# One batch of key sums per sequence, a fixed order for the first two superblocks, and later loads in a macaron transformer block

## The chip, the core and the metric

The kernel runs on one core of a Trainium2 chip. A core has five engines with instruction queues of their own: TensorE (PE; weight loads are shown as PEld), VectorE (DVE), ScalarE (ACT), GpSimd (POOL) and SyncE (SP), which issues most transfers. Engines wait for each other through semaphores. Products are accumulated in PSUM, eight banks of 128 x 2 KB. The metric is the time of one execution on the device in microseconds, the median of several runs; lower is better.

## What is computed

A macaron block over x of 16 sequences x 256 tokens x 256 features: half a feed-forward step, causal attention with 16 heads of 16 that share 4 key and value groups, and half a feed-forward step again, each on the layer norm of x and added to x. The feed-forward weights are made ternary in the kernel from their own mean absolute value.

```python
def ternary_quant(w):
    scale = jnp.mean(jnp.abs(w)) + 1e-08
    return jnp.clip(jnp.round(w / scale), -1.0, 1.0) * scale

def ffn(x):                      # W_up, W_gate: 1024 x 256, W_down: 256 x 1024
    up, gate = x @ wu.T, x @ wg.T
    return (silu(up) * gate) @ wd.T

def attn(x):
    q, k, v = x @ Wq + bq, x @ Wk + bk, x @ Wv + bv      # k, v repeated for 4 heads each
    scores = where(causal, -inf, q @ k.T / sqrt(16))
    return softmax(scores) @ v

x = x + 0.5 * ffn(layernorm(x))
x = x + attn(layernorm(x))
x = x + 0.5 * ffn(layernorm(x))
```

## The kernel before

Two sequences (512 tokens) make a superblock n = 0 to 7. All of x stays on the chip (`xs`). A pass (n, p) of the feed-forward part is eight units f of 128 hidden features, then four down products of 128 tokens each. `order` lists the sixteen passes: the first six superblocks' first pass, then second passes with the two left first passes between.

Inputs of products are split in a high and a low half-precision part, so a product u or g of a unit is four matmuls of 512 columns (`products`, L467): two halves of the features times high and low. A unit is u, g, a curve th on ScalarE (Silu for the first four passes, Tanh after), a join h on VectorE, and the split of h into hT on ScalarE (high) and GpSimd (low). `ffn_down` (L518) has sixteen matmuls of 256 columns for each 128 tokens.

The attention of a superblock: norm, transposing transfer xT_a, three products `project` (L545), the results sent to DRAM (qd, kd) and loaded again in another layout (`load(q)` for sequence q = 2n + s, four loads of queries and five of keys). `peak` scores a row's maxima, `peak_parts` and `peak_rows` turn them into three extra rows of the queries. `exponents(q, g)` (L696, L697, L705) makes for one group g of four heads three score tiles, their exponentials in a tile pT (128 x 3 x 512, three buffers) and the causal mask. `weighted(q, gp)` (L727) sums values over the keys for two groups: sixteen f32 matmuls on strips of 32 columns of the array; the profile counts 32, as f32 is done in two. `attended` (L743) turns the sums, divides by the sum of the exponentials, and GpSimd adds the result to x.

What sets the order. The program issues steps from several chains (`ffn_chain`, `prepares`, `qkv_chain`, `load_chain`, `peak_chain`, `sequence_chain`). A step has a cost, names of steps that must come before it and a lag in accumulated cost; `run` takes from the attention chains when their share of cost falls behind. The framework then orders each engine's queue by a timeline of its own, save instructions that are pinned with `keep_in_program_order` or have high priority.

At the start the weights come in and are made ternary: `ternary_sums` (absolute sums on ScalarE and VectorE), `ternary_scale` (one matmul with ones adds over the partitions, then scale, upper and lower bound), `ternary_piece` (L336 or L332 and L333: a mask below the lower bound; L337: the compare with the upper bound minus the mask). These steps are entered in `ffn_chain` at fixed places (the list at the end of the function). Filler matmuls (`warm`) come ahead of the first work (12) and of the first and third gate products (NWF, four each). The raw weights lie in the buffers that later hold the queries.

The two lines that say how the sums over the keys are laid out and issued:

```python
groups = (2 * gp, 2 * gp + 1)                 # two of the four groups of heads
steps.append([e[0], e[1], e[2], w[0], e[3], a[0], w[1], a[1]])
```

Of the kernel before, what the change touches and what calls it, by code (L numbers as in the profile page):

```python
# [25 lines left out]
ENG_U = "vvvv"  # L26
ENG_G = "vapa"
ENG_D = "aaaa"
NUF = "000000"
NWF = "404000"  # L30
# [7 lines left out]
NCUT = 4  # L38
PINF = 0
NW4 = 0  # L40
PRE = 0
USUM = 1
GSUM = 0
PING = 0
HPU = 0
GFIRST = 0
PINF1 = 0
TDA = 1
PINK = 1
KM = 2  # L50
KV = 12
PINA = 0
PINM = 1
PINT = 0
NWARM = 12
NWARM2 = 0
NWARM3 = 0
GCUT = 0
# [9 lines left out]
C1 = 1  # L68
C2 = 4
C3 = 5  # L70
TD = 6
DR = 6
DS = 2
PM = 9
LAG_NORM0 = 10.0
DOWN_AT0 = 5
DOWN_GAP0 = 1
GU = 1
QKV_LEAD = 11
LAG_ANORM = 6.0  # L80
LAG_LOAD = 12.0
GAP_PEAK = 1.0
# [11 lines left out]
NORM = 1024.0  # L94


@with_exitstack
def macaron_kernel(
# [56 lines left out]

    x_t = x.rearrange("(n s) (t p) e -> n p (s t) e", s=2, t=2)
# [39 lines left out]
    wqkv = ap_.tile([P, 3, 512], F32, tag="pT", name="wqkv", bufs=3)[:, :EC, : 3 * P]  # L196
# [4 lines left out]
    load_x(0)  # L201
    for w, w_t in ((wu, w_upT), (wg, w_gateT)):
        for i in range(NCUT if w is wu or GCUT else 1):
            nn = NCUT if w is wu or GCUT else 1
            cut = slice(i * F // nn, (i + 1) * F // nn)
            nc.sync.dma_start(w[:, :, cut], w_t.rearrange("(c p) f -> p c f", p=P)[:, :, cut])
    load_x(1)
    nc.sync.dma_start(wd, w_downT.rearrange("(c p) e -> p c e", p=P))

    def load_rest():  # L210
        nc.sync.dma_start(wqkv, w_qkv.rearrange("(c p) f -> p c f", p=P))
        nc.sync.dma_start(bqkv, b_qkv)
        for n in range(2, NSB):
            load_x(n)
# [5 lines left out]
    nc.vector.tensor_copy(identh, ident)  # L220
    ones = const.tile([P, P], F32, tag="ones", name="ones")
    nc.vector.memset(ones, 1.0)
    neg_half = const.tile([P, TT], F32, tag="neg_half", name="neg_half")
    nc.vector.memset(neg_half, -0.5)

    def warm(n, name):
        if n:
            pw = bank([P, P], f"warm_{name}")
            for _ in range(n):
                nc.tensor.matmul(pw, ones, ones, start=True, stop=True)  # L230

    warm(NWARM, "start")

# [3 lines left out]

    box = {}
# [13 lines left out]
    def constant_rows():  # L252


        c = ap_.tile([P, 2, 1536], F16, tag="pT", name="constant_rows", bufs=3)
        k, v = c[:, 0, : NU * U], c[:, 1, :P]
        nc.gpsimd.memset(k[KP:KR], 0.0)
        ku = k[KP:KR].rearrange("p (u k) -> p u k", k=U)
        for at, base in UNDER:
            nc.gpsimd.affine_select(  # L260
                out=ku[:, at : at + 2], in_=ku[:, at : at + 2], pattern=[[0, 2], [-1, U]],
                compare_op=ALU.is_ge, fill=-MASK, base=base, channel_multiplier=1,
            )
        nc.gpsimd.memset(k[KR : KR + 3], -MROW)
        nc.gpsimd.memset(v[KP:KR], 0.0)
        vj = v[KP:KR].rearrange("p (j b) -> p j b", b=4)
        nc.gpsimd.affine_select(
            out=vj, in_=vj, pattern=[[1, 32], [0, 4]], compare_op=ALU.not_equal,
            fill=MASK, base=0, channel_multiplier=-1,
        )  # L270
        for to in Ks:
            nc.sync.dma_start(
                to[KP : KR + 3].rearrange("p g u k -> p g (u k)"),
                k[KP : KR + 3].unsqueeze(1).to_broadcast([KR + 3 - KP, G, NU * U]),
            )
        box["queries"] = v

    def constant_values():
        for v in PARTS:
            nc.gpsimd.memset(v[:, 4 * 6 * G :], 0.0)  # L280
        for v in VT:
            nc.gpsimd.memset(v, 0.0)
            nc.gpsimd.memset(v[:, :, :, D : D + 1], 1.0)
# [9 lines left out]
    def ternary_sums(w, name):  # L293
        if name == "d":
            cuts = [(w[:, : FC // 2], 1), (w[:, FC // 2 :], 1)]
        elif name == "u" or GCUT:
            fq = F // NCUT
            cuts = [(w[:, :, i * fq : (i + 1) * fq], 0 if i % 2 == 0 and not USUM else 1) for i in range(NCUT - 1)]
            h = fq // 2
            cuts += [(w[:, :, (NCUT - 1) * fq : (NCUT - 1) * fq + h], 0), (w[:, :, (NCUT - 1) * fq + h :], 1)]  # L300
        else:
            cuts = [(w[:, : EC // 2], GSUM), (w[:, EC // 2 :], 1)]
        part = small.tile([P, len(cuts)], F32, tag="part", name=f"part_{name}")
        for i, (piece, on_scalar) in enumerate(cuts):
            if on_scalar:
                junk = fp.tile([P] + list(piece.shape[1:]), F16, tag="th", name=f"junk_{name}_{i}")
                nc.scalar.activation(junk, piece, AF.Abs, accum_out=part[:, i : i + 1])
            else:
                pin(PING and name == "g", nc.vector.tensor_reduce(
                    part[:, i : i + 1], piece, AX.XY, ALU.add, apply_absolute_value=True  # L310
                ))
        return part

    def ternary_scale(w, name, part):
        n = w.shape[1] * w.shape[2]
        allsum = bank([P, part.shape[1]], f"allsum_{name}")
        nc.tensor.matmul(allsum, ones, part, start=True, stop=True)
        tot = small.tile([P, 1], F32, tag="tot", name=f"tot_{name}")
        nc.vector.tensor_reduce(tot, allsum, AX.X, ALU.add)
        s = const.tile([P, 1], F32, tag=f"s_{name}", name=f"s_{name}")  # L320
        nc.vector.tensor_scalar(s, tot, 1.0 / (P * n), TERNARY_EPS, ALU.mult, ALU.add)
        hi = small.tile([P, 1], F32, tag="hi", name=f"hi_{name}")
        nc.vector.tensor_scalar(hi, s, 0.5, None, ALU.mult)
# [799 lines left out]
```

## Time and profile before

| | |
|---|---|
| median of 3 runs | 550.11 us (549.1 to 550.27) |
| the profiled execution | 550.52 us |
| its span, first to last instruction | 548.7 us |
| mean granted clock of TensorE | 0.991 |
| L518, down products | 1024 matmuls, 121.9 us busy |
| L467, u and g of most passes | 448 matmuls each, 115.3 and 115.0 us |
| L696, scores for the exponentials | 192, 54.0 us |
| L727, sums over the keys | 1024, 49.1 us (329 ns mean) |
| L697, exponentials on ScalarE | 192, 120.1 us (696 ns mean) |
| L734, copies of the sums on ScalarE | 64 of 256 elements, 22.1 us |

A row of the timeline gives the start, the duration, the engine, the line of the kernel, the operation, the output and its inputs, the shape, and how many instructions were merged; in brackets stands idle time of the engine just before, and what ended it. Durations of merged matmuls overlap those of the next row, since matmuls are pipelined: what a group costs is read from its start to the next start. In the groups, a line has the count, the busy time and the mean of one. The slices on the page are of 13.7 us each, in tenths.

### The profile page before, as it was taken

The page shows a single profiled execution, that of the slowest core. Times are in us where ns is not written, and L with a number is a line of the kernel's source. Part 1 is how long each engine was busy: PE and PEld are TensorE (multiplying, and loading weights), DVE is VectorE, ACT ScalarE, POOL GpSimd, SP SyncE. Part 2 cuts the span into 40 slices and gives each one's busy share as a digit, 9 for nine tenths or more (in the row PEclk, how much of TensorE's full clock was granted, in tenths as well). Part 3 has the DMA queues.
Part 4 walks back from the last instruction along what each step waited for, and adds up shares of the span by engine and source line. Part 5 has one row for each costly group of instructions (what it writes and reads, how often), then busy time and mean ns, then how long its engine had stood idle before and what let it go on. Part 6 is the DMA issues. An engine that isn't in the chain of part 4 may idle for free.

```text
span 548.7 us, 11537 instructions
## 1 busy us (share of the span) xinstructions
PE 530.2 (97%) x4273; PEld 328.7 (60%) x4273; DVE 434.8 (79%) x1027; ACT 375.3 (68%) x658; POOL 355.1 (65%) x384
## 2 busy tenths in 40 slices
PE   5899998989999999999999999999999999999997
PEld 4446555646655656755656656666645666566565
DVE  5988988978898899887578898678966799647753
ACT  5785847576767957797675678856698445875642
POOL 4357789656569777688555579746589443866542
PEclk7899999999999999999999999999999999999999
DMA  8923258463017527325625404660026720020201
GB/s 283 308 62 59 39 130 179 118 159 75 1 28 193 93 78 170 66 42 153 148 50 140 95 8 82 173 129 5 1 40 135 174 62 19 23 59 11 67 30 48
DMA packets 128017, 51.20 MB, mean 93 GB/s; under 512 B 102069, under 2 KB 127705, under 8 KB 127961
## 3 DMA queue, kind: packets, MB, share of 16 engines
q1 hardware_dynamic: 127529, 50.08, 38.1%
q8 instruction: 33, 0.54, 0.4%
q10 hardware_dynamic: 432, 0.39, 0.3%
q14 instruction: 23, 0.19, 0.1%
HBM read 22.41 MB, written 14.68 MB: 68 GB/s over the span
## 4 chain that ended last, share of the span: by engine, by line
PE 68%; DVE 12%; ACT 5%; DMA 5%; POOL 4%; issue 3%; SPq 2%; DVEq 0%; POOLq 0%; ACTq 0%
PE d L518 15%; PE u L467 13%; PE g L467 13%; PE o L727 8%; PE st L696 6%; PE s L630 5%; PE qkv L545 4%; DVE tops L645 2%; PE ot L743 2%; DMA qd<-sp 1%; DVE h L497 1%; DMA kd<-sp 1%; POOL hT L508 1%; ACT pT L697 1%; POOL xparts_f L383 1%
## 5 line engine op out<-in xcount | busy, mean ns | idle before, releaser
L508 POOL TENSOR_TENSOR hT<-h,hT 128x512 f16<-128x512 f32 x128 | 148.7, 1167 | 77.2 <-ACT hT L507 77.0
L697 ACT ACTIVATE pT<-st,exp_scale 128x512 f32<-128x512 f32 x192 | 120.1, 696 | 21.0 <-PE st L696 20.8
L507 ACT CAST hT<-h 128x512 f16<-128x512 f32 x128 | 79.7, 623 | 67.2 <-DVE h L502 49.1
L518 PE MATMUL d<-td,hT 128*128 128x256 f16 x1024 | 121.9, 273 | 0.5 <-DVE sp L570 0.4
L705 POOL TENSOR_SCALAR_AFFINE_SELECT pT<-pT 128x512 f32<-128x512 f32 x128 | 80.7, 636 | 58.5 <-ACT pT L697 57.8
L467 PE MATMUL u<-xT_f,tu 128*128 128x512 f16 x448 | 115.3, 379 | 0.4 <-DVE h L502 0.3
L467 PE MATMUL g<-xT_f,tg 128*128 128x512 f16 x448 | 115.0, 379 | 0.0
L645 DVE TENSOR_REDUCE tops<-s 128x8 f32<-128x512 f32 x160 | 103.4, 680 | 11.1 <-PE s L630 10.9
L518 PEld LDWEIGHTS <-hT 128*128 128x128 f16 x1024 | 98.9, 98 | 19.2 <-issue 0.9
L501 DVE SCALAR_TENSOR_TENSOR tmp<-th,u 128x512 f32<-128x512 f32 x96 | 65.7, 684 | 40.2 <-ACT th L499 39.7
L499 ACT ACTIVATE th<-u,half_u 128x512 f32<-128x512 f32 x96 | 66.6, 694 | 38.1 <-PE u L467 36.3
L467 PEld LDWEIGHTS <-tg 128*128 128x128 f16 x512 | 49.9, 98 | 63.1 <-DVE tg L337 2.9
L467 PEld LDWEIGHTS <-tu 128*128 128x128 f16 x512 | 47.1, 98 | 44.1 <-issue 2.0
L502 DVE SCALAR_TENSOR_TENSOR h<-g,tmp 128x512 f32<-128x512 f32 x96 | 65.6, 684 | 5.4 <-PE u L467 0.3
L696 PE MATMUL st<-Qs,ks 99*128 99x512 f16 x192 | 54.0, 380 | 3.4 <-ACT pT L697 2.0
L630 PEld LDWEIGHTS <-Qs 96*128 96x128 f16 x576 | 47.2, 114 | 11.6 <-issue 3.0
L630 PE MATMUL s<-ks,Qs 96*128 96x64 f16 (+3 forms) x576 | 50.2, 227 | 0.1
L727 PE MATMUL o<-pT,vt 128*32 128x128 f32 (+1 forms) x1024 | 49.1, 329 | 0.1
L523 DVE SCALAR_TENSOR_TENSOR x<-d,so,x 128x256 f32<-128x256 f32 x64 | 30.4, 477 | 20.2 <-PE d L518 19.7
L727 PEld LDWEIGHTS o<-pT,vt 128*32 128x32 f32 x1024 | 28.8, 109 | 23.9 <-issue 8.1
L383 POOL TENSOR_TENSOR xparts_f<-xn_f,xparts_f 128x1024 f16<-128x1024 f32 x14 | 29.8, 2130 | 9.6 <-ACT xparts_f L380 7.7
L545 PE MATMUL qkv<-xT_a,wparts 128*128 128x512 f16 x144 | 34.0, 379 | 1.8 <-DMA xT_a<-xparts_a 1.6
(164 smaller groups left out, 603.6 us busy)
## 6 DMA issues: line engine op xcount, KB each, us to landing
qd<-sp SPq DMA_DIRECT2D x32, 256.0 KB, 2.8
Qs<-qd SPq DMA_DIRECT2D x64, 128.0 KB, 3.6
x<-in_x SPq DMA_DIRECT2D x8, 512.0 KB, 8.8
ks<-kd SPq DMA_DIRECT2D x64, 64.0 KB, 2.7
out<-x SPq DMA_DIRECT2D x32, 128.0 KB, 2.2
kd<-sp SPq DMA_DIRECT2D x16, 128.0 KB, 2.8
ks<-kd SPq DMA_DIRECT2D x16, 128.0 KB, 2.9
Qs<-in_w_upT SPq DMA_DIRECT2D x4, 256.0 KB
```

The lines of the kernel that those rows point to most:

```text
L467: nc.tensor.matmul(acc, w[:, c, f * P : (f + 1) * P], ffn_ready[key][:, a, c, :], start=(c == 0 and a == 0), stop=(c == EC - 1 and a == 1),)
L499: nc.scalar.activation(th, up, AF.Tanh, scale=scales["half_u"])
L501: nc.vector.scalar_tensor_tensor(tmp, th, 1.0, up, ALU.add, ALU.mult)
L507: nc.scalar.copy(hT[:, f, 0, :], h)
L508: nc.gpsimd.tensor_tensor(hT[:, f, 1, :], h, hT[:, f, 0, :], ALU.subtract)
L518: nc.tensor.matmul(acc, hT[:, f, a, t * P : (t + 1) * P], td[:, f, :], start=(f == 0 and a == 0), stop=(f == FC - 1 and a == 1),)
L630: nc.tensor.matmul(sc[:, at : at + n, :], Qs[0:KR, b // 4, g * P : (g + 1) * P, b % 4], strided(k[:, g, place], [(step * U, m) for step, m ...
L645: nc.vector.tensor_reduce(peaks[q][:, u, :], sc, AX.X, ALU.max)
L696: nc.tensor.matmul(sc, keys.rearrange("p u k -> p (u k)"), mov, start=True, stop=True)
L697: nc.scalar.activation(pT[:, u, :].rearrange("p (h b j) -> p h b j", h=4, b=4), sc.rearrange("p (h j b) -> p h b j", h=4, b=4), AF.Exp, sc ...
L705: nc.gpsimd.affine_select(out=v, in_=v, pattern=[[0, 4], [1, P]], compare_op=ALU.is_ge, fill=0.0, base=0, channel_multiplier=-1,)
L727: pin(not first, nc.tensor.matmul(at[:, half * P :], v[:, 2 * s + half, g, :], moving, start=half == 0, stop=half == 1, tile_position=(0, ...
```

## The change

Three parts, each with its edits.

**Sums over the keys.** One batch `weighted(q)` takes all four groups of a sequence; two banks hold two groups each, the order inside the batch is groups 0 and 2, then 1 and 3; pT has four buffers; the copies oT take two groups at once. `sequence_chain` issues four exponent steps, the batch, and the two ends.

```diff
-        pT = ap_.tile([P, 3, 512], F32, tag="pT", name=f"pT_{q}_{g}", bufs=3)
+        pT = ap_.tile([P, 3, 512], F32, tag="pT", name=f"pT_{q}_{g}", bufs=4)
...
-    def weighted(q, gp):
+    def weighted(q):
...
-        groups = (2 * gp, 2 * gp + 1)
-        pT = [probs.pop((q, g)) for g in groups]
-        o = [bank([P, S], f"o_{q}_{g}") for g in groups]
+        pT = [probs.pop((q, g)) for g in range(G)]
+        o = [bank([P, 2, S], f"o_{q}_{gp}") for gp in range(2)]
...
+        for i2 in range(2):
+            for half in range(2):
+                for gp in range(2):
+                    g = 2 * gp + i2
+                    for i in range(4):
+                        cut = slice(i * P, (i + 1) * P)
+                        moving = pT[g][:, 0:2, cut] if half == 0 else pT[g][:, 2, cut]
+                        pin(not first, tensor.matmul(
+                            o[gp][32 * i : 32 * i + 32, i2, half * P :], v[:, 2 * s + half, g, :], moving,
+                            start=half == 0, stop=half == 1, tile_position=(0, 32 * i),
+                        ))
+                        first = False
+        for gp in range(2):
+            oT = ap_.tile([P, 2, S], F32, tag="oT", name=f"oT_{q}_{gp}", bufs=2)
+            scalar.copy(oT, o[gp])
+            sums[q, gp] = oT
...
-            steps.append([e[0], e[1], e[2], w[0], e[3], a[0], w[1], a[1]])
+            steps.append(e + [w] + a)
```

**The first two superblocks.** Everything on VectorE, ScalarE, GpSimd and TensorE up to the end of the second superblock's units, the first superblock's down products, the third superblock's norm, the split of the projection weights and the first attention norm is issued from a table of names, and each engine keeps that order (a wrapper `Engine` pins every instruction). The norm and the unit are cut into their single operations (`EarlyNorm`, `Unit`), and the making of ternary weights is changed: ScalarE writes the absolute values while it sums them (up and gate), the signs (plus or minus a half) are made before the scale is known, and one operation of VectorE compares and multiplies. For the first 256 up and gate columns it comes in two halves. The lower bound, the mask and its subtraction are gone; `HELD` carries the half in the scales. Some sums move to VectorE, all d sums stay on ScalarE. The fillers are 14 ahead of the work, then 2 and 3 inside the table; those before the gate products are gone.

```diff
+ORDER = """
+st0 ag0 st1 rs0 ag1 su0 xn0 rs1 su1 gu0:V tr0 gu1:P xn1 tr1 warm2 gu2:V su2 su3v hi01 gu3:P hi00
+lo01 allu warm3 azu lo00 sg0 oneu cutu peru tu0b tu0a gg2:P U01 sg1 gg0:V tu2 azg U00 th01 tu1
+gg3:P s1b U03 th00 s1a U02 sg1v th03 gg1:P agg1 allg gd3:A tu3 U04 gd2:A cutg misc gd0:A tg3 U07
+rs1x gd1:A tg0b tg0a G01 sd0 tg2 sh1 xV G00 xA1 h01 xA0 G05 tg1 th02 h00 H01 G03 s2a L01 H00 G02
+h03 th04 L00 U05 h02 H03 th07 G04 s2b L03 H02 tr1x th05 h04 L02 G06 h05 hi11 hi10 G07 lo11 H05
+lo10 U06 H04 L05 h07 sd1 U10 most L04 U11 th06 H07 h06 U13 th11 L07 ag2 mt th10 alld G11 ve2 top
+H06 miscd rs2 cutd td1 th13 ev U16 L06 xV2 G17 sh2 h11 xA2 td3 G10 H11 td2 G13 ph2 L11 td0 U17 h10
+th16 pl2 D1 h13 H10 pw H13 th17 D2 L10 END2 h17 ws us L13 D0 H17 r2 wc L17 sa2 D3 r1 wl r0 sa1 sa0
+U14 r3 sa3 G16 th14 aga G12 rsa h16 U15 H16 sha xVa xAa L16 G15 G14 pha U12 h14 th15 pla h15 H14
+th12 H15 h12 ENDa L15 H12 L14 L12
+"""
...
+            def issue(*args, **kwargs):
+                ins = fn(*args, **kwargs)
+                if box["in_order"]:
+                    tc.keep_in_program_order(ins)
+                return ins
...
+    def size_pass(n, c, lo, hi, i=None):
+        scalar.activation(
+            size[n][:, c, lo:hi], raws[n][:, c, lo:hi], AF.Abs,
+            **({} if i is None else {"accum_out": part[n][:, i : i + 1]}),
+        )
...
+    def sums_by_vector(n, c, lo, hi, i):
+        vector.tensor_reduce(
+            part[n][:, i : i + 1], raws[n][:, c, lo:hi], AX.X if isinstance(c, int) else AX.XY, ALU.add, apply_absolute_value=True
+        )
...
+    def half_sign(engine, n, cut):
+        if engine is scalar:
+            scalar.activation(sign[n][cut], raws[n][cut], AF.Sign)
+        else:
+            engine.tensor_scalar(sign[n][cut], raws[n][cut], 0.0, 0.5, ALU.is_ge, ALU.subtract)
...
+    def ternary(n, cut):
+        src = size[n] if n in size else raws[n]
+        vector.scalar_tensor_tensor(tern[n][cut], src[cut], cuts[n], sign[n][cut], ALU.is_gt, ALU.mult)
...
+    by = {"V": vector, "P": gpsimd, "A": scalar}
+    for name in ORDER.split():
+        if name[:4] == "warm":
+            warm(int(name[4:]))
+            continue
+        name, _, engine = name.partition(":")
+        ops[name](*([by[engine]] if engine else []))
+    box["in_order"] = False
+    constant_keys()
```

How to read the table. `Ukf`, `Gkf`: up and gate product of unit f of superblock k; `th`, `h`, `H`, `L`: its curve (ACT), join (DVE), high (ACT) and low (POOL) part. `st`, `ag`, `rs`, `xn`, `tr`, `hi`, `lo`: the first superblock's norm by halves; `s1..`, `xA`, `xV`, `tr1x`: the second's; `s2..` to `END2`: the third's; `sa` to `ENDa`: the first attention norm. `su`, `sg`, `sd`: sums of sizes; `allu`, `allg`, `alld`: the sum over the partitions; `gu0:V`: signs of a quarter of the up weights on VectorE (P: GpSimd, A: ScalarE); `tu`, `tg`, `td`: the ternary weights; `D`, `r`: down product and residual; `most` to `us`: the projection weights.

The loads at the start: x of the first superblock in two halves, the gate weights in two halves instead of one transfer, the rest in the same succession. The vt memsets go from GpSimd to VectorE; the constant rows of the keys are sent after the table (`constant_keys`), those of the queries at place 12 of the chain. In the tanh path the product (th + 1) u is written over th, where it went to a tile of its own.

**Loads of the second sequence.** An odd sequence's loads come a lag after the even one's, for sequence 1 also after the norm of the second superblock's attention; its transposing transfer and those loads are pinned.

```diff
-            need = [(("project", q // 2, 1), 3.0)]
+            need = [(("load", q - 1), LAG_ODD)] if q % 2 else [(("project", q // 2, 1), 3.0)]
+            if q == 1:
+                need.append((("anorm", 1), 1.0))
...
+            pin(name == "a_1", nc.sync.dma_start(xT, parts.rearrange("p a c t e -> p (a c t e)"), transpose=True))
```

`LAG_ODD` is 5. `run` counts the table's feed-forward cost as done when it starts.

## The prediction

> **What bounds the kernel now.** I read the page's busy shares and slices first, to see which engine sets the end and where it is not full.
>
> ```profile
> span 548.7 us, 11537 instructions
> PE 530.2 (97%) x4273; PEld 328.7 (60%) x4273; DVE 434.8 (79%) x1027; ACT 375.3 (68%) x658; POOL 355.1 (65%) x384
> PE   5899998989999999999999999999999999999997
> DVE  5988988978898899887578898678966799647753
> PEclk7899999999999999999999999999999999999999
> ```
>
> TensorE is the bound. From the fourth slice on it is full, so there a change pays only by making TensorE's own work shorter or by taking out a wait of TensorE. The first two slices (13.7 us each) are the only stretch with much idle time, at a reduced clock. Asked by stage, PE is busy 48.13 of the first 57.00 us, 64.02 of 57 to 125, and 372.75 of the 375 us from 125 to 500.
>
> Next, TensorE's timeline of the start.
>
> ```profile
> 9.64 0.59 PE L317 MATMUL allsum_u<-part_u,ones 128*128 128x5 f32 x2 [4.26 <-ACT junk_u L307]
> 11.19 2.03 PE L402 MATMUL xt_first<-ident,xn_first 128*128 128x128 f32 x8 [0.96 <-ACT xn_first L363]
> 13.94 0.61 PE L467 MATMUL u<-xT_first,tu 128*128 128x512 f16 x1
> 14.34 1.92 PE L230 MATMUL warm_g<-ones 128*128 128x128 f32 x8
> 16.05 1.49 PE L467 MATMUL u<-xT_first,tu 128*128 128x512 f16 x3
> 18.69 1.04 PE L467 MATMUL g<-xT_first,tg 128*128 128x512 f16 x4 [1.15 <-DVE tg L337]
> 24.70 1.03 PE L467 MATMUL u<-xT_first,tu 128*128 128x512 f16 x4
> 55.90 1.03 PE L467 MATMUL g<-xT_second,tg 128*128 128x512 f16 x4
> ```
>
> The first product starts at 13.94 and waits in the middle of its four matmuls until 16.05; at 24.70 only three units (six products of four matmuls, u and g of each) are done; the last product of the second superblock starts at 55.90 and the next group starts at 56.76. A product costs 0.863 us at full clock (24.70 to 25.56), so six are 5.2 us.
>
> VectorE's timeline of the same stretch says why.
>
> ```profile
> 13.14 0.74 DVE L337 SCALAR_TENSOR_TENSOR tu<-Qs,hi_u,dn_u 128x512 f16<-128x512 f32 x1
> 13.80 1.40 DVE L348 BATCH_NORM_STATS2 st_second<-x 128x6 f32<-128x256 f32 x4
> 15.11 0.67 DVE L405 TENSOR_TENSOR xT_first<-xt_first,xT_first 128x512 f16<-128x512 f32 x1
> 17.89 0.74 DVE L337 SCALAR_TENSOR_TENSOR tg<-Qs,hi_g,dn_g 128x512 f16<-128x512 f32 x1
> ```
>
> The low part of the first input (L405) runs after work that nobody needs yet: the statistics of the second superblock, and ahead of them 1.20 us of gate sums at 12.02.
>
> Then the sums over the keys in the timeline of TensorE, whole and split:
>
> ```profile
> 123.40 1.03 PE L467 MATMUL g<-xT_f,tg 128*128 128x512 f16 x4
> 124.36 1.51 PE L727 MATMUL o<-pT,vt 128*32 128x256 f32 x32
> 125.80 0.82 PE L696 MATMUL st<-Qs,ks 99*128 99x512 f16 x3
> ```
> ```profile
> 309.22 1.29 PE L727 MATMUL o<-pT,vt 128*32 128x256 f32 x24
> 310.44 0.39 PE L696 MATMUL st<-Qs,ks 99*128 99x512 f16 x1
> 310.76 0.43 PE L727 MATMUL o<-pT,vt 128*32 128x128 f32 x8
> 311.12 0.60 PE L696 MATMUL st<-Qs,ks 99*128 99x512 f16 x2
> ```
>
> A product ends its share of the array at 123.40 + 0.863 = 124.26; the batch starts 0.10 later and the next group starts 1.44 after it: 1.54 us for a batch. Nearly all 32 batches show these numbers. In the split batch, 8 short matmuls cost 0.10 + 0.36 and the other 24 cost 0.10 + 1.22, so a split costs 1.78 - 1.54 = 0.24 us: an entry and an exit are a fixed price, whatever is in the batch.
>
> Last, the queue of loads and the one wait of TensorE on a transfer:
>
> ```profile
> 87.47 4.24 SPq L613 DMA_DIRECT2D ks<-kd  x5
> 91.82 2.25 SPq L388 DMA_TRANSPOSE xT_a<-xparts_a  x1
> ```
> ```profile
> 96.21 1.47 PE L545 MATMUL qkv<-xT_a,wparts 128*128 128x512 f16 x6 [1.58 <-DMA xT_a<-xparts_a]
> ```
>
> **The change, part by part.** The sum starts from the profiled execution: 550.52 us, of which 548.7 are its span; it is 0.41 above the median of the runs, 550.11.
>
> *One batch per sequence.* 32 batches become 16 of twice the matmuls; the same matmuls run, so 16 entries and exits go. By the split batch one is 0.24; a second reckoning: if 32 matmuls alone took the time of their columns at the pace of L467 (512 columns in 0.216 us, four passes for f32, four column strips at once) they took 2 x 0.43 + 2 x 0.215 = 1.29, and 1.54 - 1.29 = 0.25. I take 0.25: **-4.0 us**. Bounds: the visible entry alone, 16 x 0.10 = -1.6; and -4.8, if the three split batches (0.24 each) come whole too. The 64 copies oT (390 ns for 256 elements) become 32 of 512, near the 623 to 696 ns of other ACT passes of 512: 22.1 us become some 21, on an engine at 68%. Nothing there.
>
> *The table of the first two superblocks.* I walked the table engine by engine, each strictly in its order, with the row durations above. The last quarter of the up weights is there at 9.01 (the start of L309). VectorE sums 512 elements: between 0.42 (256) and 1.20 (1024), 0.65, to 9.7. The transposes need both halves of x normalised: 8.6 on VectorE (statistics 4 x 0.34, 1.0 us of power on POOL, four passes of 0.34, one sign of 0.48 between), then four transposes at half clock, 0.9, to 9.6; two high parts on ACT to 10.8; the low parts (0.67) end at 11.8; four scales of 0.07 to 0.15 and a half ternary of 0.37 follow: the first product starts at **12.6**, with its input whole. In before it ran from 16.05. Then VectorE issues, up to the first gate weights: 0.36 + 0.48 + 2 x 0.67 + 1.36 + 0.62 + 0.4 + 0.67 + 0.42 + 0.67 + 0.36 = 6.7, so the first gate product starts at **19.3**, while PE does six up products (5.2 us, and up to 3 more if the clock is still low). So six products are done at 19.3 where before had six at 24.70: 5.4 us won. From there 26 products (22.4), eight transposes (0.87), 64 down matmuls (7.0) and 0.6 of small ones are 30.9. Before needed 32.06 for it, 1.2 of it waits. In my walk VectorE is the tight engine up to 28 us (joins of 0.67, ternaries of 0.67, statistics) and PE waits 1.9: the second superblock ends at 52.2 in place of 56.76, or at 52.7 if the clock stays low until 17.6. **-4.3 us.** Bounds: no wait behind the first gate product and no low clock, 18.9 + 30.9 = 49.8, so -7.0; on the other side the fixed order makes a late transfer hold a whole queue. ACT takes the signs of the down weights at 18.6 with the curves behind them; before's first use of those weights, junk_d at 19.71, found them there, so the hold is at most 1.1: -3.2. If VectorE's waits come twice, 1.9 more: -1.3. The removed filler (warm_g, 16 passes) is in the walk already.
>
> The clock in this case: the slice from 7.00 to 7.50 is the first below 1.00 (0.84), the one from 17.50 to 18.00 the first above 0.50 (0.92), while PE last worked at 5.38 before the fall. The Trainium skill ("TensorE: Matmul & The Clock Gate", section "Part 1: The HAM clock gate") says that the clock falls only after an idle window of about 3.4 us, free-running. The row shows the fall 1.9 us after the last filler, so the measurement decides; by the rule the longer filler here would keep the full clock, and the table would end at 52.2; by the row it is low from 7.3 on and the end is 52.7.
>
> *Moved constants.* Memsets of vt go from POOL (3 x 0.52) to VectorE: hidden before x arrives, since L348 waited 1.56 for it; without that cover 1.2. POOL's constant rows (3.3 us, done at 5.2) now stand ahead of the power at 5.6: hidden by 0.4. Three ks constants (3.58 us of issues, before at 18.84) go behind the table's transfers; the first reader is the scores at 87: hidden.
>
> *Second sequence's loads later.* In before ten or eleven issues (83.40 to 91.71) stand ahead of the transpose of xT_a on SP's queue, and PE waits 1.58. Now the transpose goes first: **-1.6**. Behind the loads then stands the transpose of xT_f (96.56), later by up to 8; its superblock starts on PE some 10 us after that, so I cost it at nothing, and at up to 1 without that cover. The loads' scores begin at 106.5 in before, 15 us after the last issue; LAG_LOAD keeps 12 of it. Bounds -1.6 to 0.
>
> *Waits that the new shape may add.* All four tiles of exponentials are now full when the batch starts, and the tanh path holds th through two operations. The rows' waits of PE behind ACT's pT are 1.44 and 0.51 in the whole run. I add **+0.4**, one wait as the smaller; bounds 0 and 16 x 0.25 = +4.
>
> Sum: 550.52 - 4.0 - 4.3 - 1.6 + 0.4 = 541.0, and 0.4 lower on the scale of the median: **540.6 us**.
>
> **Rivals.** *The start is set elsewhere* (transfers, or VectorE, which is busy in 46.50 of the first 57 us): the early gain is given back by 57 us, the rest stays: 550.1 - 4.0 - 1.6 = 544.5. For it: DVE's slices 9 8 8 at the start. Against: L405 waits for order, not for data. 15%.
>
> *The start gains all it can*: -7.0, whole batches -4.8, and -1.6, with half of the 4.3 us of other PE waits after 97 gone too (-2.2): 534.5. For it: waits such as 1.44 at 117.90 come from the short ring of pT. Against: VectorE in the walk. 15%.
>
> *The batches are split anyway*: the instructions' order still lets a score group in between, as in 3 of 32 now. If each of 16 is split once, the 4.0 go: 544.6, 8%.
>
> *The single batch starves TensorE* (slower): the next sequence's exponentials can't start before the batch has read the first tile; their st banks stay full, and score groups queue behind them on PE. Its price is the row at 117.90, 1.44 a sequence: 15 x 1.44 = 21.6, so 550.1 - 9.5 + 21.6 = 562. It decides from 9.5 / 15 = 0.63 us a sequence. For it: four tiles for four groups leave none spare. Against: the batch takes groups 0 and 2 first, and feed-forward products lie between. 10%.
>
> **Chances and range.** The forecast has 0.48, with its own range 537.5 to 543.5; the rivals 0.15, 0.15, 0.08 and 0.10; 0.04 is left for no change. What this kernel's measurement can tell from none is 0.2%, 1.1 us. Faster: 0.86; same 0.04; slower 0.10. The range takes in the second and third cases and the wide end of the added waits: 534.5 to 548.
>
> **What would show it.** First u product near 12.6 and the last of the second superblock near 52.5; L727 in 16 groups of x64 of about 2.72 from start to next start; no wait of qkv on xT_a near 92; PE idle from 125 to 500 not above some 3 us. It is wrong if PE waits for ACT's pT in each sequence, if L727 comes in pieces, or if the table's end lies past 55.

## The result, and the profile after

The changed kernel takes 554.4 us (median of 4 runs, 553.62 to 555.62) beside 550.18 for the kernel before on the same chip: a ratio of 1.0083, 95% interval 1.006 to 1.0106. It is slower, by some 4 us; 540.6 was forecast. The profiled execution took 554.08 us.

The page's head and slices of the changed kernel:

```profile
span 552.4 us, 11442 instructions
PE 529.8 (96%) x4283; PEld 330.3 (60%) x4283; DVE 435.4 (79%) x1030; ACT 369.6 (67%) x618; POOL 361.8 (65%) x383
PE   8999998989999999999999999999969999999997
PEclk9999999999999999999999999999989999999999
```

TensorE has no more work than before (529.8 us busy, before 530.2), and the first slices are fuller (8 and 9; before 5 and 8). But the thirtieth slice, 400 to 414 us, shows 6 for PE and the only 8 in the row of the clock. Before, both stood at 9 there.

TensorE's timeline at the places that the prediction named, and in that slice. In the changed kernel every recorded operation carries the line of the wrapper, L151, so rows are told apart by their tiles.

```profile
12.19 1.90 PE L151 MATMUL u<-xT_first,tu 128*128 128x512 f16 x8 [0.82 <-DVE tu L151]
...
52.12 1.03 PE L151 MATMUL u<-xT_f,tu 128*128 128x512 f16 x4
...
89.45 1.47 PE L151 MATMUL qkv<-xT_a,wparts 128*128 128x512 f16 x6 [2.41 <-DMA xT_a<-xparts_a]
...
371.48 2.81 PE L151 MATMUL o<-pT,vt 128*32 128x256 f32 x64
374.22 0.64 PE L151 MATMUL s<-ks,Qs 96*128 96x128 f16 x8
...
403.23 2.59 PE L151 MATMUL o<-pT,vt 128*32 128x256 f32 x56
405.75 0.40 PE L151 MATMUL pt<-identh,parts 128*128 128x128 f16 x4
406.89 0.42 PE L151 MATMUL o<-pT,vt 128*32 128x128 f32 x8 [0.74 <-POOL pT L151]
411.29 6.61 PE L151 MATMUL qkv<-xT_a,wparts 128*128 128x512 f16 x18 [3.97 <-DMA xT_a<-xparts_a]
417.83 0.46 PE L151 MATMUL v<-ident,full 64*128 64x64 f32 x4
```

The start is as the prediction walked it: first product at 12.19, third superblock's first product at 52.12 (before 56.76). The single batch has the predicted size: 371.48 to 374.22. Then, at the projections of the last superblock, TensorE stands for 0.74 and 3.97 us, and the 18 matmuls that follow take 6.54 us (411.29 to 417.83). The same 18 take 3.98 in another run below. In before there is no wait at this place, six of them take 1.3 us, and other work follows between the projections:

```profile
409.33 1.03 PE L467 MATMUL g<-xT_f,tg 128*128 128x512 f16 x4
410.19 1.46 PE L545 MATMUL qkv<-xT_a,wparts 128*128 128x512 f16 x6
411.48 0.38 PE L743 MATMUL ot<-ident,oT 128*128 128x128 f32 x2
```

To see where time goes, count the matmul work done, each group at its full-clock pace, and compare the moments at which the two kernels have done the same amount. This is the changed kernel's lead over before, worked out from both timelines and good to about half a microsecond:

| at (time of before, us) | 57 | 123 | 217 | 311 | 389 | 421 | 527 |
|---|---|---|---|---|---|---|---|
| lead, us | +4.65 | +3.9 | +2.7 | +4.0 | +4.25 | -4.3 | -3.9 |

The start wins 4.65, three hundred microseconds of sequences win next to nothing more, and one place loses 8.5. What follows asks why there, and why the sequences brought nothing.

The windows of the changed kernel about that place (start and end, length, then busy time and instructions of PE, PEld, DVE, ACT and POOL, granted clock, share of the DMA engines, GB/s):

```profile
380.00:405.00 25.00, 23.67 (x192) 14.30 (x194) 23.76 (x61) 17.33 (x29) 15.33 (x18) 1.00 0.01 2
405.00:411.30 6.30, 1.58 (x33) 0.77 (x26) 4.54 (x6) 4.60 (x8) 5.50 (x6) 0.87 0.59 88
411.30:418.00 6.70, 6.70 (x20) 2.49 (x21) 1.92 (x4) 3.48 (x5) 4.05 (x3) 0.61 0.54 100
```

PE does 1.58 us of work in 6.30, the clock falls inside the idle stretch, and most of the projections run at a mean clock of 0.61. VectorE is busy for 23.76 of the 25 us before: it is the tight engine there, though only 79% busy over the span.

The chain of waits of the changed kernel, in order of time (start, duration, what):

```profile
393.04 0.71 POOL pT L151
393.75 0.98 POOL rstd_a L151
394.73 0.98 POOL rstd_f L151
395.72 0.60 POOL pT L151
396.32 1.15 POOL hT L151
397.48 0.74 POOL x L151
398.21 0.59 POOL pT L151
398.80 0.69 POOL x L151
...
404.11 2.14 POOL xparts_a L151
406.24 0.03 POOL pT L151
406.27 4.97 DMA xT_a<-xparts_a
411.24 0.05 issue
411.29 6.61 PE qkv L151 x18
```

Read it backwards. The projections waited for the transposed input xT_a, that for GpSimd's split xparts_a at 404.11, and GpSimd had a queue of other things ahead of it: masks of the exponentials pT, residuals x, a split hT, another norm's power. Nothing in this chain is a batch of sums over the keys; it is the last superblock's attention norm, late.

VectorE's timeline of the changed kernel, where that norm begins:

```profile
388.62 0.47 DVE L151 SCALAR_TENSOR_TENSOR x<-d,out_scale,x 128x256 f32<-128x256 f32 x1
389.01 1.28 DVE L151 TENSOR_REDUCE tops<-s 128x8 f32<-128x512 f32 x2
390.21 0.42 DVE L151 BATCH_NORM_STATS2 st_a<-x 128x6 f32<-128x256 f32 x1
...
393.15 0.11 DVE L151 TENSOR_SCALAR ve_a<-mv_a 128x4 f32<-128x4 f32 x1
```

The maxima `tops` of another sequence's scores, 0.6 us or more each, stand between the last residual and the statistics that need it, and more operations of other chains, two more maxima among them, follow before ve_a at 393.15.

### The profile page after: what moved, and what is told of

Read it like the earlier page. It is cut to its first block, busy times and chain, and to the rows that moved or that the text cites. A ratio compares the mean times of both kernels' runs of the same rounds, so it can differ in the third digit from the quotient of the medians.

```text
span 552.4 us, 11442 instructions
## 1 busy us (share of the span) xinstructions
PE 529.8 (96%) x4283; PEld 330.3 (60%) x4283; DVE 435.4 (79%) x1030; ACT 369.6 (67%) x618; POOL 361.8 (65%) x383
## 4 chain that ended last, share of the span: by engine, by line
PE 76%; DVE 8%; DMA 5%; POOL 4%; ACT 4%; issue 1%; SPq 1%; ACTq 0%; POOLq 0%; DVEq 0%
PE d L151 19%; PE g L151 16%; PE u L151 15%; PE o L151 7%; PE qkv L151 6%; PE st L151 5%; PE s L151 5%; DMA xT_a<-xparts_a 2%; PE ot L151 2%; DVE tops L151 1%; ACT pT L151 1%; DMA Qs<-in_w_upT 1%; POOL pT L151 1%; DVE h L151 1%; DVE xn_f L151 1%
## 5 line engine op out<-in xcount | busy, mean ns | idle before, releaser
L151 POOL TENSOR_TENSOR hT<-h,hT 128x512 f16<-128x512 f32 x128 | 148.8, 1167 | 120.1 <-ACT hT L151 120.1
L151 ACT CAST hT<-h 128x512 f16<-128x512 f32 x128 | 79.7, 624 | 71.4 <-DVE h L151 70.9
L151 ACT ACTIVATE pT<-st,exp_scale 128x512 f32<-128x512 f32 x192 | 119.6, 698 | 7.2 <-PE st L151 6.1
L151 PE MATMUL d<-td,hT 128*128 128x256 f16 x1024 | 121.9, 273 | 1.0 <-DVE td L151 1.0
L151 PE MATMUL u<-xT_f,tu 128*128 128x512 f16 x448 | 115.1, 379 | 2.7 <-DVE sp L151 2.0
L151 DVE TENSOR_REDUCE tops<-s 128x8 f32<-128x512 f32 x160 | 102.9, 678 | 16.7 <-PE s L151 16.6
L151 PE MATMUL g<-xT_f,tg 128*128 128x512 f16 x448 | 115.2, 379 | 0.0
L151 PEld LDWEIGHTS <-hT 128*128 128x128 f16 x1024 | 98.6, 98 | 21.1 <-DVE td L151 1.5
L151 DVE SCALAR_TENSOR_TENSOR th<-th,u 128x512 f32<-128x512 f32 x96 | 65.5, 683 | 40.7 <-ACT th L151 40.1
L151 ACT ACTIVATE th<-u,half_u 128x512 f32<-128x512 f32 x96 | 66.7, 696 | 38.8 <-PE u L151 38.2
L151 POOL TENSOR_SCALAR_AFFINE_SELECT pT<-pT 128x512 f32<-128x512 f32 x128 | 79.9, 634 | 18.5 <-ACT pT L151 17.5
L151 PEld LDWEIGHTS <-tg 128*128 128x128 f16 x512 | 49.9, 98 | 61.1 <-DVE tg L151 1.7
L151 PEld LDWEIGHTS <-tu 128*128 128x128 f16 x512 | 47.7, 98 | 52.7 <-issue 5.3
L151 DVE SCALAR_TENSOR_TENSOR h<-g,th 128x512 f32<-128x512 f32 x96 | 65.6, 686 | 5.3
L151 PE MATMUL st<-Qs,ks 99*128 99x512 f16 x192 | 52.8, 378 | 3.0 <-ACT pT L151 1.6
L151 PEld LDWEIGHTS <-Qs 96*128 96x128 f16 x576 | 47.9, 114 | 9.9 <-issue 1.5
L151 PE MATMUL s<-ks,Qs 96*128 96x64 f16 (+3 forms) x576 | 50.1, 226 | 0.1
L151 PE MATMUL o<-pT,vt 128*32 128x128 f32 (+1 forms) x1024 | 46.0, 328 | 0.7 <-POOL pT L151 0.7
L151 DVE SCALAR_TENSOR_TENSOR x<-d,out_scale,x 128x256 f32<-128x256 f32 x64 | 30.4, 478 | 17.7 <-PE d L151 17.2
L151 PE MATMUL qkv<-xT_a,wparts 128*128 128x512 f16 x144 | 36.9, 400 | 6.7 <-DMA xT_a<-xparts_a 6.4
L151 POOL TENSOR_TENSOR sp<-full,sp 128x512 f16<-128x512 f32 (+1 forms) x24 | 27.6, 1154 | 21.7 <-DVE sp L151 21.6
L151 PEld LDWEIGHTS o<-pT,vt 128*32 128x32 f32 x1024 | 29.3, 110 | 18.7 <-issue 4.7
```

What stands on the lines that cost most here:

```text
L151: ins = fn(*args, **kwargs)
```

## The experiments

All times are medians, with the ratio to the kernel before on the same chip and its 95% interval. No kernel here leaves out any of the computation.

**Two batches again, table and later loads kept.** The changed kernel with two batches per sequence and three buffers of exponentials.

```diff
-        pT = ap_.tile([P, 3, 512], F32, tag="pT", name=f"pT_{q}_{g}", bufs=4)
+        pT = ap_.tile([P, 3, 512], F32, tag="pT", name=f"pT_{q}_{g}", bufs=3)
...
-            steps.append(e + [w] + a)
+            steps.append([e[0], e[1], e[2], w[0], e[3], a[0], w[1], a[1]])
```

> The changed kernel with the sums over the keys as before (two batches a sequence, three buffers of exponentials); table and later loads stay. Theory B (the single batch empties TensorE's queue near 405 us, where the last superblock's transpose is awaited): the 4.6 us won by the table survive, some 546 us, and TensorE waits under 1.5 us for the last xT_a. Theory L (any lead of TensorE is lost there, because the norms on ScalarE, VectorE and GpSimd set that place): the lead shrinks to nothing at 405 to 420, some 550 us.

546.59 us, 0.9941 (0.9926 to 0.9955): faster than both kernels. The single batch, forecast at -4.0 and +0.4 for its waits, costs 7.8 us in this company. The lead over before is 5.2 at 57 us (the third superblock's first product starts at 51.53, in before at 56.76), 4.1 at 405 and 3.7 at 527: nothing is lost at 405 to 418. The projections in its TensorE timeline:

```profile
404.90 1.03 PE L151 MATMUL g<-xT_f,tg 128*128 128x512 f16 x4
405.76 1.46 PE L151 MATMUL qkv<-xT_a,wparts 128*128 128x512 f16 x6
407.05 0.38 PE L151 MATMUL ot<-ident,oT 128*128 128x128 f32 x2
407.27 0.81 PE L151 MATMUL st<-Qs,ks 99*128 99x512 f16 x3
407.92 0.38 PE L151 MATMUL ot<-ident,oT 128*128 128x128 f32 x2
408.14 1.46 PE L151 MATMUL qkv<-xT_a,wparts 128*128 128x512 f16 x6
```

No wait, and the scores and turned sums of the running sequences lie between the projections. In the changed kernel those had all been done earlier, and the three projections stood in a row with nothing behind which to hide.

**Loads together again, single batch and table kept.** The loads of a superblock's second sequence follow its first sequence's at once, and the pins of the first of them are gone.

```diff
-            need = [(("load", q - 1), LAG_ODD)] if q % 2 else [(("project", q // 2, 1), 3.0)]
-            if q == 1:
-                need.append((("anorm", 1), 1.0))
+            need = [(("project", q // 2, 1), 3.0)]
```

> The changed kernel with the second sequence's loads as before (no lag, nothing pinned); table and single batch stay. Theories B and L: the wait near 411 stays (4 us and a low clock after it), 553 to 556 us. Rival (the later loads move the attention so that nothing is left to do near 405): under 550 us.

559.79 us, 1.0174 (1.0154 to 1.0193), outside both bounds given: the later loads are worth 5.4 us here, where the prediction had 1.6.

**The table alone.** Both edits above together: two batches, loads together.

> The changed kernel with both the sums over the keys and the loads as before, so the table and the start alone. Theory B: 545 to 547 us. Theory L: 549 to 551 us. If the loads do harm besides the batch, faster than with the later loads by 1 us or more.

552.54 us, 1.0045 (1.003 to 1.006): neither theory. The start alone wins 4.45 us by 57 us, and the kernel is slower all the same. Against the first experiment, the later loads are worth 6.0. SyncE's queue and TensorE of this run, in two fences:

```profile
80.72 3.98 SPq L649 DMA_DIRECT2D Qs<-qd  x6
84.74 4.20 SPq L656 DMA_DIRECT2D ks<-kd  x5
89.05 1.97 SPq L356 DMA_TRANSPOSE xT_a<-xparts_a  x1
```
```profile
93.65 2.74 PE L151 MATMUL qkv<-xT_a,wparts 128*128 128x512 f16 x6 [6.42 <-DMA xT_a<-xparts_a]
96.18 1.06 PE L151 MATMUL s<-ks,Qs 96*128 96x256 f16 x7
```

GpSimd had xparts_a ready at 84.53 (started 82.39, 2.14 long), but the transpose is issued at 89.05, behind eleven loads. TensorE, early by its start, waits 6.42 us where before waited 1.58, and the next six matmuls and the group behind them run slowly (2.53 us from start to start; 1.30 in the row at 89.45 of the changed kernel). The lead goes from 4.5 at 87 us to -1.3 at 123. With the later loads SyncE issues the transpose first, in the changed kernel's queue:

```profile
84.34 3.04 SPq L356 DMA_TRANSPOSE xT_a<-xparts_a  x1
87.43 2.60 SPq L649 DMA_DIRECT2D Qs<-qd  x4
```

and TensorE still waits 2.41, because now the norm itself, done at 84.3, is the limit.

**The batch alone on the kernel before.** It needs room for the fourth buffer: with that buffer and nothing else changed there is no kernel to time, as a pool of 32 KB per partition has 26.4 KB left. I made the room by writing the tanh product over th and putting the start's masks in the ring of h.

```diff
-            tmp = fp.tile([P, 512], F32, tag="tmp", name=f"tmp_{name}")
-            nc.vector.scalar_tensor_tensor(tmp, th, 1.0, up, ALU.add, ALU.mult)
+            nc.vector.scalar_tensor_tensor(th, th, 1.0, up, ALU.add, ALU.mult)
...
-            steps.append([e[0], e[1], e[2], w[0], e[3], a[0], w[1], a[1]])
+            steps.append(e + [w] + a)
```

> The kernel before with the single batch and four buffers of exponentials (the tanh product written over th and the start's masks in another ring, to make room). Theory Q (the single batch piles the scores, exponentials and masks of two sequences onto the last superblock's attention norm, whose transpose TensorE then awaits; TensorE's lead plays no part): slower, 555 to 559 us, TensorE idle 3 us or more ahead of the last three projections, and these at half clock. Rival L2 (it takes the lead of the table as well to reach that wait): 546 to 549 us. The saved entries alone, if nothing else changed, would be -4.

568.36 us, 1.0342 (1.0316 to 1.0369): worse than either theory, but most of it isn't the batch's. The new order or the making of room disturbed the start (waits of PE of 2.46 us at 32.66 and 4.93 at 78.23), well ahead of the first sums over the keys: the run is 12.3 us behind before at 87 us and 12.4 at 405, and the sequences between cost nothing and gain nothing. Then comes the event again:

```profile
427.06 5.38 PE L544 MATMUL qkv<-xT_a,wparts 128*128 128x512 f16 x18 [4.20 <-DMA xT_a<-xparts_a]
```

It loses some 6 us more. So the loss at the last projections comes with the batch, whether TensorE is ahead or behind (the norm's times, in the table below, are those of the changed kernel); the size of the whole run says nothing on the batch.

**Only the first loads later.** The first experiment with the second sequence's loads delayed for sequence 1 alone.

```diff
-            need = [(("load", q - 1), LAG_ODD)] if q % 2 else [(("project", q // 2, 1), 3.0)]
+            need = [(("project", q // 2, 1), 3.0)]
```

> As a1_two_batches, but of the later loads only sequence 1 keeps its condition and its pins; the lag of the other odd sequences is gone. Theory S (what the later loads bring is the one transpose at 84 us that no longer stands behind eleven loads on SP's queue): 546 to 547.5 us, as a1. Rival (the lag of the other sequences counts): 549 us or more.

546.89 us, 0.9943 (0.9928 to 0.9958), the same as with all loads later (546.59): so with two batches the one transpose near 84 us is all that this part is about.

**Later loads alone on the kernel before.** The same condition and pins, no other part.

> The kernel before with the second sequence's loads later, alone. By my prediction -1.6 us (the wait of 1.58 on the second transpose): 548 to 549 us. Theory S (the loads in SP's queue set the time of that transpose, and TensorE's arrival sets how much of it is seen): the same 1.6 here, while with the table it was 6.0. Rival (the later loads help elsewhere, in the steady part): under 546 us.

549.53 us, 0.9987 (0.9972 to 1.0003): no clear difference, where both theories had 1.6. In the profiled execution the wait of 1.58 is gone and some 2 us are won by 98 us, but nearly all of it is given back by 123 us: 0.65 by the v product's wait for a ScalarE copy at 99.86, 0.49 by a wait at 115.96, and the rest by a low clock from 118.45 to 121.87, behind a wait of 1.44 that before has too, there at the full clock. With the runs above this settles the part: nothing that can be told from none alone, 5.4 to 6.0 us behind the table.

**The peaks of sequence 13 later, all parts of the change kept.** Its scores, whose maxima stood on VectorE ahead of the norm's statistics, may only be issued after the last superblock's projections.

```diff
+                if q == 2 * NSB - 3 and u == 0:
+                    need.append((("project", NSB - 1, 1), 0.0))
```

> The changed kernel whole, with one more condition: the scores for the maxima of sequence 13 are issued after the last superblock's projections. Theory Q (the last attention norm is late because VectorE, ScalarE and GpSimd are given the scores, exponentials and masks of sequences 12 and 13 at the same time): its transpose is issued 4 us or more sooner after the down products, TensorE waits under 1 us for it, 545 to 548 us. Rival (the wait is TensorE's own: no product is left to do there, whatever the norm does): 552 us or more.

548.79 us, 0.9981 (0.9969 to 0.9994): 5.6 us better than the changed kernel and better than before, though 0.8 above the band of theory Q. TensorE's timeline:

```profile
400.76 0.81 PE L151 MATMUL st<-Qs,ks 99*128 99x512 f16 x3
401.50 4.04 PE L151 MATMUL qkv<-xT_a,wparts 128*128 128x512 f16 x18
405.48 0.85 PE L151 MATMUL o<-pT,vt 128*32 128x256 f32 x12
```

The same 18 matmuls in a row, without a wait and in 3.98 us. The lead over before stays near 4 until 497 us; then a new wait of 1.32 on xT_f at 514.60 takes it to 2.7.

**The exponentials of sequence 12 later.** The other load on the norm's window, instead of the peaks.

```diff
+            if q == 2 * NSB - 4:
+                e[0].after = list(e[0].after) + [(("project", NSB - 1, 1), 0.0)]
```

> The changed kernel whole, with one more condition: the exponentials of sequence 12 are issued after the last superblock's projections; the scores of 13 stay where they were. Theory Q, if the exponentials and masks on ScalarE and GpSimd are the pile: 545 to 548 us. If the scores on VectorE are the pile: the wait stays, 551 us or more.

553.41 us, 1.0054 (1.0037 to 1.0071): almost nothing is mended.

```profile
407.53 6.77 PE L151 MATMUL qkv<-xT_a,wparts 128*128 128x512 f16 x18 [4.70 <-DMA xT_a<-xparts_a]
```

The norm of six kernels side by side, from the timelines (end of the last down products: the start of TensorE's next group; then starts on GpSimd and SyncE, and the first projection):

| us | down products end | rstd_a | xparts_a | transpose | from first to transpose | projections start |
|---|---|---|---|---|---|---|
| before | 396.60 | 398.37 | 403.39 | 405.55 | 9.0 | 410.19, no wait |
| two batches | 392.17 | 393.94 | 398.96 | 401.12 | 9.0 | 405.76, no wait |
| changed | 388.00 | 393.72 | 404.11 | 406.27 | 18.3 | 411.29 after 3.97 |
| peaks later | 386.76 | 388.58 | 393.32 | 395.48 | 8.7 | 401.50, no wait |
| exponentials later | 388.12 | 393.34 | 399.51 | 402.74 | 14.6 | 407.53 after 4.70 |
| batch alone | 403.50 | 409.27 | 419.65 | 421.81 | 18.3 | 427.06 after 4.20 |

From the down products to rstd_a is VectorE's part: 1.8 us where it is free, 5.2 to 5.8 with four maxima of sequence 13 ahead. From rstd_a to xparts_a is ScalarE's and GpSimd's part: 4.7 to 5.0, 10.4 with eight of sequence 12's twelve exponentials in between (the other four stand ahead of rstd_a), 6.2 with them moved. In before, three of them stand there. Taking the exponentials out alone gives back 4 us of the norm's time, but TensorE then runs out of other work at 402.83 and waits as long as before the edit. The edit on the peaks moved more than the peaks: in that run no exponential of sequence 12 is left between the down products and xparts_a either. So it clears both piles at once, and what the peaks cost by themselves is read from the two runs together, 14.6 against 8.7 us.

**Seven units ahead.** AHEAD, the number of first passes ahead of the first second pass, from 6 to 7, on the changed kernel:

```diff
-AHEAD = 6
+AHEAD = 7
```

> The changed kernel with seven first passes ahead in place of six, so that the last superblock's first pass and its attention norm come a pass earlier, away from that pile. Theory Q: the wait at the last projection goes, 8 us with its low clock, 545 to 548 us. Rival (the single batch costs time all over the run): 552 us or more.

548.5 us, 0.9981 (0.9966 to 0.9996), half a microsecond above what was expected. The wait at the last projections is gone: 0.44 at 383.40, and on `tops`. But waits of about 1 us of u on VectorE's sp appear at 162.09, 206.57, 250.87 and 295.37. The same constant on the kernel with two batches:

> As a1_two_batches (table, later loads, two batches) with seven first passes ahead: the control for b2. Theory Q: nothing to mend there, 545 to 548 us, so that b2 against b3 shows what the single batch saves where it does no harm: by the entries 2 to 4 us for the single batch, by the rival nothing or a loss.

553.79 us, 1.0082 (1.0057 to 1.0108): missed, 7 us worse than with six, by waits in many places, the longest 2.27 of st on pT at 216.62, behind which the clock is low for 3.4 us. So the pair doesn't isolate the batch, as it was meant to: the constant moves every engine's queue, and what it does to one kernel says nothing of the other. Why it costs two batches 7 us stays open.

## Why the prediction was wrong

The sum was 550.52 - 4.0 - 4.3 - 1.6 + 0.4. By its own steps:

**The table, -4.3: right.** 4.64 us at the third superblock's first product, which starts at 52.12 for 52.2; the first product at 12.19 for 12.6, the first gate product at 19.24 for 19.3. The walk, engine by engine in strict order, was good to half a microsecond. The rival "the start is set elsewhere" falls. The clock stayed full to 57 us from 6.89 on, where its record begins (28 fillers from 1.10 take 6.14 us, four from 8.46 take 0.45). Fillers and transposes followed on each other with hardly a gap, so this execution doesn't test the fall that before showed after 1.9 us. Three other runs with the same table (loads together, table alone, seven ahead with two batches) had the clock low for 3.4 us from 11.8 to 12.2 us on, and a lead of 4.1 to 4.4 us at the third superblock's first product; the other six had 4.6 to 5.2.

**The batch, -4.0: its price right, its count a little off.** A batch takes 2.74 us and an entry of 0.10, 2.84, against twice 1.54 = 3.08: 0.24 for each exit and entry saved. Five of the 16 batches are split by another group (one at 403.23), as three of 32 were: 21 entries for 35, so 14 x 0.24 = 3.4 us. That work is gone. Ten of the 14 lie between 123 and 389 us (26 in before, 16 here), 2.4 us, yet the lead grows there by 0.35 only. New waits of PE ate most of the rest: u on sp 0.95 at 205.19 and 1.06 at 249.71, and several of 0.2 to 0.4. Busy time of PE from 125 to 500 us was 365.36 (before 372.75), so 9.6 us idle where the prediction allowed 3; 4.7 of that are the two waits of the event.

**The later loads, -1.6: the wrong kind of term.** In before 1.58 us of wait lay there, and I subtracted it beside the table's 4.3 as if the two were independent. But a TensorE that comes 4.6 us earlier to the same transpose waits longer for it. With the loads in front it waits 6.42 and the lead is lost; with them behind it waits 2.41 (1.68 with two batches), as the norm's own chain sets the end. The 1.6 never arrived; instead this part lets the table keep what it won. Table and loads together gave 3.6 (546.59 against 550.18) of the 5.9 forecast.

**The failed step: "Waits that the new shape may add."** It reads "The rows' waits of PE behind ACT's pT are 1.44 and 0.51 in the whole run. I add **+0.4**, one wait as the smaller; bounds 0 and 16 x 0.25 = +4." I looked only at the wait that the batch's own operands could cause, and at a size per sequence. That wait stayed much as it was (1.10 and 0.51, near 114 and 118 us). What came instead is one event of 8.5 us: 0.74 + 3.97 of waiting, 2.6 of projections at a low clock, and 1.3 more of waits in the 25 us before. Its cause, shown by clearing the norm's window (peaks later, 5.6 us back), by the two-batch run (7.8) and by the batch alone, where the norm takes the same 18.3 us: with the batch after four groups of exponentials, the order of steps changes so that sequence 13's maxima and all of sequence 12's exponentials fall on VectorE, ScalarE and GpSimd in the window of the last attention norm, which doubles from 9.0 to 18.3 us, while TensorE has used up the groups that in before lie ahead of and between the projections. My bounds could not contain it, and so neither could the range, whose upper end was 548.

**The rival "the single batch starves TensorE"** had the sign and the part right, and its mechanism wrong: not 1.44 in each sequence for the lack of a spare tile, but a transfer that is late once. My 10% for it was one price and one place; the same edit had other ways to be slower, and I gave those nothing.

What stays open: the batch without side effects was not isolated, nor which part of its edit moves the maxima and exponentials (the later place of the sums, the fourth buffer, the new costs and lags of the steps). Single batch with the peaks moved is 548.79, two batches 546.59. The two profiled executions are 1.4 us apart (547.82 and 546.39), near the one wait of 1.32 at 514.60; no version with the single batch came below 546.59. That a better order could keep it is possible and not shown. Of the versions run, the table with later loads and two batches is the best, 546.59 (546.89 with only the first loads later, no clear difference).

## What to carry to other kernels

Where a step changes the order in which chains are issued, don't only ask what the step itself waits for: list which operations move, on every engine, in front of the next chain that TensorE must wait for, and how much work TensorE has left to cover that chain. A gain ahead of a wait is worth only what the wait lets through, so terms on both sides of one transfer are not added; find what limits the transfer once the engine comes earlier. An engine that is 79% busy on average can be the bound for 25 us, and a hand-off that falls there is where a small saving turns into a loss.

## What the runs showed of the hardware

A wait of TensorE can cost more than its length, by the clock that follows it. In the changed kernel the clock falls at 409.66 and is back at 416.48; both moments are worked out from the mean clock of one-microsecond windows, with 1.00 and 0.50 as the only two values. In the same way:

| run | idle of PE ahead (us) | clock low from | to | for |
|---|---|---|---|---|
| before, at the start | 5.38 to 9.64 | 7.34 | 17.58 | 10.2 |
| loads together | 6.38 | 90.74 | 97.56 | 6.8 |
| changed, at 411 | 3.97 | 409.66 | 416.48 | 6.8 |
| exponentials later | 4.70 | 406.24 | 413.06 | 6.8 |
| batch alone | 4.20 | 426.36 | 429.78 | 3.4 |
| seven ahead, two batches | 2.14 | 90.58 | 94.0 | 3.4 |
| changed, at 89 | 2.41 | not | | |
| two batches, at 88 | 1.68 | not | | |

The low spells here are one, two or three times 3.4 us long; the longest on record, at the start of the later loads alone and of the batch alone, is four times (13.65). Idle of 2.14 us lost the clock where 2.41 kept it, so the length of the wait alone doesn't decide. Windows of the run with seven ahead and two batches, columns as above, where TensorE worked until 87.55 and from 89.69 on:

```profile
89.00:90.00 1.00, 0.31 (x2) 0.20 (x3) 0.93 (x3) 0.47 (x1) 1.00 (x1) 1.00 0.63 143
90.00:91.00 1.00, 1.00 (x6) 0.37 (x5) 1.00 (x3) 0.66 (x2) 1.00 (x2) 0.79 0.74 170
91.00:92.00 1.00, 1.00 (x6) 0.62 (x5) 1.00 (x3) 1.00 (x3) 1.00 (x2) 0.50 1.01 211
...
94.00:95.00 1.00, 1.00 (x11) 0.75 (x10) 1.00 (x3) 0.39 (x1) 0.00 (x0) 1.00 0.45 102
```

The clock falls at 90.58, 0.9 us after the work came back. In the 3.4 us up to that fall PE was busy for 1.3 (0.4 and 0.9), and in the 3.4 us up to the fall at 7.34 in before for 1.45.

In each of the twelve profiled runs the moments at which the clock changes lie whole multiples of 3.413 us apart. Cut into such stretches, their timelines from 23 us on show the full clock lost after every stretch in which TensorE was busy for 1.48 us or less (1.48 in the later loads alone, 115.04 to 118.45), and after none with 1.65 or more (1.65 in the changed kernel, 85.39 to 88.81; 1.73 in two batches, 86.33 to 89.75). So by these rows the same wait costs a low spell or not by where it falls in the stretch, and executions of one kernel differ: the four of the changed kernel have mean clocks of 0.994, 0.994, 0.991 and 0.988, at 554.08, 553.62, 554.72 and 555.62 us. The fall 1.9 us after the last filler that puzzled the prediction fits this. The low spells near 12 us don't: there the clock fell after stretches with 2.3 to 2.5 us of transposes, small sums and fillers, and in other runs stayed after as much, so what decides there stays open.

The Trainium skill's page "TensorE: Matmul & The Clock Gate", section "Part 1: The HAM clock gate (the "warmup" mystery)", has a free-running window of about 3.4 us that decides on the clock. The lengths of the spells agree with it; but read as a full window of idleness the rule would have spared the run with 2.14, and the measurement says that a window with more than a third of work in it (1.3 and 1.48 of 3.41 us) can lose the clock too.

An entry into and exit from the 128 x 32 mode of the array cost 0.24 us (0.10 in, about 0.14 out), in two independent reckonings: split batches of before, and whole batches of after. The skill's page "TensorEngine Tiling (Array Packing)", section "Key Properties", says that a change of mode drains the engine, with no price for it; this is one.

In the table alone, eleven loads issued ahead of a transpose took 8.3 us of SyncE's queue (80.72 to 89.05); the transpose, whose input was ready at 84.53, waited through the last 4.5 of it. A transpose took 4.4 to 5.3 us from its issue to the start of the projection that waited for it (91.82 to 96.21 in before; 84.34 to 89.45 and 406.27 to 411.29 in the changed kernel; 421.81 to 427.06 in the batch alone).
